# A graph attention layer on one core: the prologue as a written-out pipeline, the output in fifteen parts inside the batch loop, and the merge flags in PSUM

## The chip, the cores and the metric

One core of one Trainium2 chip runs the kernel; the other cores are idle. The metric is device time in microseconds (us) of one execution: the median of repeated runs without the profiler. One further execution was recorded by the hardware profiler, and every duration below that has a line beside it comes from that one.

The engines of the core have names used throughout: PE (matrix multiply, with its weight loads PEld), DVE (vector), ACT (scalar and activation), POOL (GpSimd) and SP (sync, here only a queue for DMA transfers). SBUF is the on-chip memory, PSUM the accumulator memory beside PE.

## The reference

A layer of graph attention with four heads of 32 columns over 12,500 nodes and 412,500 edges, sorted by their target `dst`:

```python
h = relu(layernorm(x))                          # 12500 x 128
hw = (h @ W_node.T).reshape(N, 4, 32)           # projected rows
e = (edge_attr_64 @ W_edge.T).reshape(E, 4, 32)
att = sum(concat([hw[src], hw[dst], e], -1) * a, -1)
att = where(att > 0, att, 0.2 * att)            # E x 4
m = maximum(segment_max(att, dst), 0)
ex = exp(att - m[dst])
denom = segment_sum(ex, dst) + (E - deg) * exp(-m)
out = x + segment_sum(ex / denom[dst] * hw[src], dst)
```

The term `(E - deg) * exp(-m)` counts every edge that does not end in the node as a zero.

## The kernel before

The kernel has three stages that follow each other.

**Prologue.** The 12,500 rows of `x` are handled as 98 blocks of 128 nodes (`NB`), seven blocks at a time (`GB`, lines L276 to L314): load, mean and variance (L289, L290), `rstd` and `shift` (L292 to L295), normalize with ReLU on ACT (L302), transpose on PE (L304) and copy to SBUF on DVE (L306), multiply by the weights on PE (L309), copy to `rows` on ACT (L310), write a constant one and keep the target's term `tn` on DVE (L312, L313), store 140 columns a node into the DRAM tensor `table` (L314). The same stage prepares tables on the edges. An edge chunk is 896 edges; there are 461 of them, padded to 464 (`NC2`). Its smallest target and whether it is sorted go through `ext` (L206 to L223), then some thirty DVE instructions on 464 columns make `floor`, `q0`, `new`, `lastm` and `nid` (L225 to L262), and POOL makes `key`, the place of each edge's target inside a window of 32 nodes, for all 3,248 columns at once (L265 to L274). A scheduler chooses the order on each engine here.

**Batches.** 58 batches (`NBT`) of eight chunks. In this stage the order is written by hand (`tc.manual_schedule()`), and each engine runs its own instructions strictly in that order. For batch b+1, POOL issues one indirect DMA for each tile of 128 edges (L364, `gather`), 3,223 in all, each fetching 128 rows of `table` into `hs`. They are issued in three groups a batch; a one-column POOL copy named `gate` (L360) makes each group wait until DVE and ACT have come to a certain point of batch b: the copy of chunk group 0 or 2 by ACT (L458), or the copy `r` (L473). For batch b, `weigh` (L402 to L426) makes the attention weights on DVE and ACT, `scatter` (L442 to L449) multiplies the gathered rows and sums them by target on PE; `begin` of batch b+1 (L377 to L396) compares targets (`mem`), multiplies the edge features (L382, L385) and builds the one-hot matrices `hot` from `key` (L393). After every second batch `merge` (L475 to L523) joins sixteen chunk results into the accumulator `acc` on DVE. SP loads each batch's edge features, targets and small tables.

**Rest.** `count_windows`, called in batch 3, counts the chunks that did not fit a window; a loop at the end (`window`, L794) redoes them, and runs no round on these inputs. Then `em` (L802 to L807) and, seven blocks at a time, `wgt`, PE, the sum with `x` and the store (L808 to L833) make the output.

Of the kernel before, what the change touches and what calls it, by code (L numbers as in the profile page):

```python
# [9 lines left out]
F32 = mybir.dt.float32  # L10
BF16 = mybir.dt.bfloat16
I32 = mybir.dt.int32
# [5 lines left out]
P = 128  # L18
# [23 lines left out]
GB = 7  # L42
FH = 2 * H
# [17 lines left out]
def filled(sc):  # L61

    return [T if c < NCH - 1 else LAST for c in (2 * sc, 2 * sc + 1) if c < NCH]

# [10 lines left out]
def kernel(  # L75
# [32 lines left out]
    key = const.tile([P, COLS], BF16, name="key")  # L108
    acc = const.tile([P, NQ, AW], F32, name="acc")
    nc.gpsimd.memset(acc, 0.0)  # L110
# [38 lines left out]
    def index(b):  # L149
        t = indices.tile([P, SB * CT], I32, name="src")  # L150
        nc.sync.dma_start(t, src[:, b * SB * CT:(b + 1) * SB * CT])
        return t

    early = [index(b) for b in range(2)]


    with (
        tc.tile_pool(name="prep1", bufs=1) as p1,
# [10 lines left out]
        dsts = p1.tile([P, COLS], I32, name="dsts")  # L169
        nc.scalar.dma_start(dsts, dst)  # L170
# [35 lines left out]
        for g in range(NG):  # L206
            n = min(P, NC2 - g * P)
            dch = p2.tile([P, CE], I32, name="dch")
            nc.sync.dma_start(dch[:n, :], dstc[g * P:g * P + n, :])
            nc.vector.tensor_reduce(ext[:n, g, 0:1], dch[:n, :], AX.X, OP.min)  # L210
            rise = p2.tile([P, CE - 1], I32, name="rise")
            nc.gpsimd.tensor_tensor(rise[:n, :], dch[:n, 1:], dch[:n, :CE - 1], op=OP.subtract)
            nc.vector.tensor_reduce(ext[:n, g, 1:2], rise[:n, :], AX.X, OP.min)
            pen = p2.tile([P, CE + 1], F32, name="pen")
            nc.gpsimd.memset(pen, -BIG)
            nc.vector.tensor_scalar(pen[:n, 1:CE], rise[:n, :], 0.0, -BIG, op0=OP.not_equal, op1=OP.mult)
            nc.sync.dma_start(pens[g * P:g * P + n, :], pen[:n, :])
        pb = [pps.tile([P, NC2], F32, name=f"pb{k}", bufs=1) for k in range(2)]
# [14 lines left out]

        floor = p1.tile([P, NC2], F32, name="floor")
# [24 lines left out]
        for a in range(4):  # L259
# [5 lines left out]
        dl = p1.tile([P, COLS], I32, name="dl")  # L265
        nc.vector.tensor_scalar(dl, dsts, W - 1, None, op0=OP.bitwise_and)
        rel = p1.tile([P, COLS], F32, name="rel")
        nc.gpsimd.tensor_copy(rel, dsts)
        nc.gpsimd.tensor_tensor(rel.rearrange("p (c t) -> p c t", t=T), rel.rearrange("p (c t) -> p c t", t=T),
                                floor[:, :, None].to_broadcast([P, NC2, T]), op=OP.subtract)  # L270
        nc.gpsimd.tensor_scalar(rel, rel, float(W), float(W), op0=OP.is_ge, op1=OP.mult)
        low_f = p1.tile([P, COLS], F32, name="dsts")
        nc.gpsimd.tensor_copy(low_f, dl)
        nc.gpsimd.tensor_tensor(key, rel, low_f, op=OP.add)  # L274

        for b0 in range(0, NB, GB):  # L276
            xg = p2.tile([P, GB, D], F32, name="xg")
            n = min(GB, -(-(N - b0 * P) // P))
            full = min(n, (N - b0 * P) // P)
            nc.sync.dma_start(xg[:, :full, :],  # L280
                              x[b0 * P:(b0 + full) * P, :].rearrange("(b p) d -> p b d", p=P))
            if full < n:
                nc.vector.memset(xg[:, full, :], 0.0)
                rest = N - (b0 + full) * P
                nc.sync.dma_start(xg[:rest, full, :], x[(b0 + full) * P:N, :])
            mv = p2.tile([P, GB, 2], F32, name="mv")
            for i in range(GB):
                stats = p2.tile([P, 6], F32, name="stats")
                nc.vector.bn_stats(stats, xg[:, i, :])  # L289
                nc.vector.bn_aggr(mv[:, i, :], stats)  # L290
            rstd = p2.tile([P, GB], F32, name="rstd")
            nc.scalar.activation(rstd, mv[:, :, 1], AF.Sqrt, bias=eps)  # L292
            nc.vector.reciprocal(rstd, rstd)
            shift = p2.tile([P, GB], F32, name="shift")
            nc.vector.scalar_tensor_tensor(shift, mv[:, :, 0], -1.0, rstd, op0=OP.mult, op1=OP.mult)  # L295
            rows = p2.tile([P, GB, ROW], F32, name="rows")
            for i0 in range(0, GB, 3):
                m = min(3, GB - i0)
                pt = pps.tile([P, 3, P], F32, name="pt")
                for i in range(i0, i0 + m):  # L300
                    hn = p2.tile([P, D], F32, name="hn", bufs=3)
                    nc.scalar.activation(hn, xg[:, i, :], AF.Relu, scale=rstd[:, i:i + 1],  # L302
                                         bias=shift[:, i:i + 1])
                    nc.tensor.transpose(pt[:, i - i0, :], hn, ident)  # L304
                hT = p2.tile([P, 3, P], F32, name="hT")
                nc.vector.tensor_copy(hT[:, :m, :], pt[:, :m, :])  # L306
                ph = pps.tile([P, 3, ROW], F32, name="ph")
                for i in range(m):
                    nc.tensor.matmul(ph[:, i, :], hT[:, i, :], wall, start=True, stop=True)  # L309
                nc.scalar.copy(rows[:, i0:i0 + m, :], ph[:, :m, :])  # L310
                ones = rows[:, i0:i0 + m, FH:].rearrange("p b (h k) -> p b h k", h=H)[:, :, :, HD]
                nc.vector.memset(ones, 1.0)  # L312
                nc.vector.tensor_copy(tn[:, b0 + i0:b0 + i0 + m, :], ph[:, :m, H:FH])  # L313
            nc.scalar.dma_start(table[b0 * P:(b0 + GB) * P, :].rearrange("(b p) c -> p b c", p=P), rows)  # L314


# [5 lines left out]
    bank = ps.tile([P, 2 * T * R + W], F32, name="exr")  # L322
    exr = [bank[:, k * T * R:(k + 1) * T * R].rearrange("p (t r) -> p t r", t=T) for k in range(2)]
    rows_ps = bank[:, 2 * T * R:]
# [48 lines left out]
    def begin(s):  # L373
# [9 lines left out]
        for part in (slice(0, HALF), slice(HALF, CE)):  # L383
            for k in range(2):
                nc.tensor.matmul(s.z[:, part], twb[:, s.b % 2, k, :], s.mem[:, k, part], start=False,  # L385
                                 stop=(k == 1))
        s.hot = []
        for j in range(SB):
            sc = s.b * SB + j
            if not tiles_of(sc):  # L390
# [3 lines left out]
                                    key[:, sc * CT:(sc + 1) * CT, None].to_broadcast([P, CT, W]),  # L394
# [80 lines left out]
    def merge(g, n):  # L475
# [34 lines left out]
        here = lastm[:, c0:c0 + n, :]  # L510
# [14 lines left out]
    def count_windows():  # L525
# [23 lines left out]
        nc.vector.tensor_copy(total, sum_f)  # L549
# [9 lines left out]

    with tc.manual_schedule():  # L560
        for b in range(-1, NBT):
            if b == -1:
                for k in range(2):
                    batch(k).src = early[k]
                load_pen(batch(0))
            elif b + 2 < NBT:
                batch(b + 2).src = index(b + 2)
# [8 lines left out]
            if b >= 0:  # L576
                s = batch(b)
                weigh(s)
                if b + 1 < NBT:
                    load_pen(batch(b + 1))  # L580
                s.pas = work.tile([P, BUF], F32, name="m")[:, :CB * H * AW].rearrange("p (c k) -> p c k", c=CB)
# [14 lines left out]
            if b == 3:  # L596
                count_windows()
    stack.close()
# [5 lines left out]
    neg_big = work.tile([P, 1], F32, name="neg_big")  # L604
    nc.vector.memset(neg_big, -BIG)
    ones = work.tile([1, P], F32, name="ones")
    nc.vector.memset(ones, 1.0)

    rsum = work.tile([P, P // W, W], F32, name="rsum")
    nc.vector.tensor_copy(rsum, rsame[:, None, :].to_broadcast([P, P // W, W]))  # L610

    tq = work.tile([P, NQ], F32, name="tq")
    for s in range(P // W):
        ptn = ps.tile([P, NB], F32, name="pz")
        for h in range(H):
            nc.tensor.matmul(ptn[h * W:(h + 1) * W, :], ident[s * W:(s + 1) * W, s * W:(s + 1) * W],
                             tn[s * W:(s + 1) * W, :, h], start=True, stop=True,
                             tile_position=(s * W, h * W))
        nc.vector.tensor_copy(tq.rearrange("p (b s) -> p b s", s=P // W)[:, :, s], ptn)

    def window():
# [9 lines left out]
        for i, row in enumerate([left_row] + rows):  # L631
# [6 lines left out]
                                       op0=OP.mult, op1=OP.add)  # L638
        vals = work.tile([1, 3], I32, name="vals")
        nc.vector.tensor_scalar(vals[:, 0:1], first, -1.0, float(NSC), op0=OP.mult, op1=OP.add)  # L640
# [151 lines left out]

    windows = nc.values_load(total[0:1, 0:1], min_val=0, max_val=NCH * NQ)
    with tc.For_i(0, windows, 1):  # L794
        window()


    stack.close()
    work = ctx.enter_context(tc.tile_pool(name="fin", bufs=2))
    ps = ctx.enter_context(tc.tile_pool(name="fin_ps", bufs=2, space=bass.MemoryType.PSUM))  # L800
    em = work.tile([P, NQ], F32, name="em", bufs=1)
    nc.scalar.activation(em, acc[:, :, AW - 1], AF.Exp, scale=-1.0)  # L802
    rest = work.tile([P, NQ], F32, name="rest", bufs=1)
# [65 lines left out]
```

## Time and profile before

| what | value |
|---|---|
| median of 3 runs | 5097.42 us (5096.45 to 5098.61) |
| profiled execution, own time | 4340.74 us |
| its span, first to last instruction | 4339.0 us |
| POOL busy | 3162.1 us (73%) |
| DVE busy | 1756.9 us (40%) |
| PE busy | 1260.8 us (29%) |
| ACT busy | 453.5 us (10%) |
| DMA moved | 434.48 MB |

The profiled execution is 756.68 us shorter than the median of the runs. Shares of busy time are averages over the three stages, which are limited by different things; the timeline is what separates them. DMA issue is not counted as busy, except that POOL's indirect DMAs are, since POOL works on each of them.

### The profile page before, as it was taken

The page shows a single profiled execution, that of the slowest core. Times are in us where ns is not written, and L with a number is a line of the kernel's source. Part 1 is how long each engine was busy: PE and PEld are TensorE (multiplying, and loading weights), DVE is VectorE, ACT ScalarE, POOL GpSimd, SP SyncE. Part 2 cuts the span into 40 slices and gives each one's busy share as a digit, 9 for nine tenths or more (in the row PEclk, how much of TensorE's full clock was granted, in tenths as well). Part 3 has the DMA queues.
Part 4 walks back from the last instruction along what each step waited for, and adds up shares of the span by engine and source line. Part 5 has one row for each costly group of instructions (what it writes and reads, how often), then busy time and mean ns, then how long its engine had stood idle before and what let it go on. Part 6 is the DMA issues. An engine that isn't in the chain of part 4 may idle for free. (4 is left out here: it accounts for less than half of the span.)

```text
span 4339.0 us, 30729 instructions
## 1 busy us (share of the span) xinstructions
PE 1260.8 (29%) x9107; PEld 535.4 (12%) x9107; DVE 1756.9 (40%) x3136; ACT 453.5 (10%) x1430; POOL 3162.1 (73%) x3422
## 2 busy tenths in 40 slices
PE   3613131313232222313131323232232313131324
PEld 2301010101011110101010101111010101010101
DVE  7325343444334342534343433434253434343346
ACT  2301010100101010101010000101010101010010
POOL 5277777777777777777777777777777777777771
PEclk8556565656555655556565656565655656565655
DMA  3433433333343334343343434343434333343434
GB/s 96 139 91 94 112 106 93 105 91 109 86 110 85 109 86 109 86 108 103 93 106 89 110 87 110 85 110 86 109 85 109 96 99 104 90 108 88 109 86 129
DMA packets 235471, 434.48 MB, mean 100 GB/s; under 512 B 85642, under 2 KB 135814, under 8 KB 235174
## 3 DMA queue, kind: packets, MB, share of 16 engines
q0 software_dynamic: 103136, 231.23, 23.5%
q1 hardware_dynamic: 118678, 192.44, 13.5%
q10 hardware_dynamic: 13488, 8.82, 0.6%
q8 instruction: 73, 1.20, 0.1%
q14 instruction: 96, 0.79, 0.1%
HBM read 417.15 MB, written 15.09 MB: 100 GB/s over the span
## 5 line engine op out<-in xcount | busy, mean ns | idle before, releaser
L364 POOL DMA_INDIRECT hs<-table,src x3223 | 3072.6, 953 | 1067.5 <-issue 1043.4
L449 PE MATMUL pa<-rhs,hot 128*32 128x140 f32 x6448 | 516.8, 430 | 2900.8 <-DVE rhs L444 2888.2
L402 DVE STREAM_TRANSPOSE zst<-hs 128x224 f32<-128x224 f32 x58 | 23.9, 412 | 1867.0 <-DMA hs<-table,src 1867.0
L449 PEld LDWEIGHTS pa<-rhs,hot 128*32 128x32 f32 x6448 | 271.4, 152 | 3148.3 <-issue 2740.1
L444 DVE TENSOR_TENSOR rhs<-hs,exr 128x924 f32<-128x924 f32 x461 | 515.0, 1117 | 151.2 <-ACT rhs L442 151.2
L382 PE MATMUL z<-eft,wa 128*32 128x384 f32 (+1 forms) x928 | 433.2, 627 | 16.2 <-DMA twb<-table 16.2
L411 ACT ACTIVATE a<-z 32x224 f32<-32x224 f32 x232 | 80.5, 347 | 2057.6 <-DVE z L410 2057.6
L385 PE MATMUL z<-mem,twb 128*32 128x512 f32 x464 | 186.7, 546 | 3.9 <-DMA twb<-table 3.9
L382 PEld LDWEIGHTS z<-eft,wa 128*32 128x32 f32 x928 | 119.1, 128 | 305.9 <-issue 300.1
L442 ACT COPY rhs<-exr 128x28 f32<-128x28 f32 x461 | 97.9, 212 | 332.3 <-DVE rhs L444 276.9
L420 ACT ACTIVATE both<-a 32x224 f32<-32x224 f32 x232 | 89.9, 388 | 376.3 <-DVE a L417 372.0
L393 DVE TENSOR_TENSOR hot<-exr,key 128x448 f32<-128x448 f32 x231 | 127.5, 611 | 0.0
L523 DVE TENSOR_TENSOR acc<-acc,a 128x70 f32 x461 | 109.7, 238 | 34.3 <-DVE acc L523 19.6
L458 ACT COPY m<-pa 128x280 f32<-128x280 f32 x231 | 90.5, 392 | 310.9 <-PE pa L449 310.9
L410 DVE TENSOR_TENSOR z<-z,zst 32x224 f32<-32x224 f32 x232 | 89.8, 387 | 77.9 <-ACT a L411 71.9
L416 DVE TENSOR_TENSOR_SCAN m<-pen,up 32x896 f32<-32x896 f32 x58 | 116.4, 2008 | 7.8 <-DVE up L414 0.5
L414 DVE TENSOR_TENSOR_SCAN up<-pen,z 32x896 f32<-32x896 f32 x58 | 117.0, 2017 | 2.0
L485 DVE TENSOR_SCALAR mc<-r 128x16 f32<-128x16 f32 (+1 forms) x29 | 5.6, 192 | 249.1 <-ACT r L473 249.1
L377 DVE TENSOR_SCALAR mem<-mem,nid 128x896 f32<-128x896 int32 x116 | 81.2, 740 | 26.3 <-DMA mem<-in_dstc 26.3
L422 DVE SCALAR_TENSOR_TENSOR both<-pen,m 32x224 f32<-32x224 f32 x232 | 88.7, 382 | 2.4
L473 ACT COPY r<-t 128x280 f32<-128x280 f32 (+1 forms) x58 | 23.7, 409 | 592.3 <-PE z L385 591.4
L467 PE MATMUL t<-m,rsame 128*32 128x280 f32 (+1 forms) x464 | 73.4, 415 | 0.4 <-ACT m L458 0.4
(142 smaller groups left out, 994.9 us busy)
## 6 DMA issues: line engine op xcount, KB each, us to landing
eft<-in_ef SPq DMA_DIRECT2D x58, 1792.0 KB
mem<-in_dstc SPq DMA_DIRECT2D x116, 448.0 KB
hs<-table,src POOLq DMA_INDIRECT x3223
xg<-in_x SPq DMA_DIRECT2D x26, 448.0 KB
twb<-table SPq DMA_DIRECT2D x464, 0.5 KB
table<-rows ACTq DMA_DIRECT2D x14, 490.0 KB
pen<-pens SPq DMA_DIRECT2D x58, 112.1 KB
out<-o SPq DMA_DIRECT2D x13, 448.0 KB
```

Source lines behind the costliest of these rows:

```text
L364: nc.gpsimd.indirect_dma_start(out=s.hs[:, i, :], out_offset=None, in_=table[:, :], in_offset=bass.IndirectOffsetOnAxis(ap=s.src[:, i:i + ...
L382: nc.tensor.matmul(s.z[:, part], wa3[:, j, :], s.eft[:, j, part], start=(j == 0), stop=False)
L385: nc.tensor.matmul(s.z[:, part], twb[:, s.b % 2, k, :], s.mem[:, k, part], start=False, stop=(k == 1))
L393: nc.vector.tensor_tensor(hot, rows_ps[:, None, :].to_broadcast([P, CT, W]), key[:, sc * CT:(sc + 1) * CT, None].to_broadcast([P, CT, W]), ...
L414: nc.vector.tensor_tensor_scan(up, s.pen[:, :CE], s.z, 0.0, op0=OP.add, op1=OP.max)
L416: nc.vector.tensor_tensor_scan(m[:, ::-1], s.pen[:, CE:0:-1], up[:, ::-1], 0.0, op0=OP.add, op1=OP.max)
L420: nc.scalar.activation(both[g * R:(g + 1) * R, 0, :, :], grouped(att, g), AF.Exp)
L442: nc.scalar.copy(rhs[:, :n, :, HD + 2], s.mx[:, :n, q * H:(q + 1) * H])
L444: nc.vector.tensor_tensor(rhs[:, :n, :, :HB], s.hs[:, i0:i0 + n, FH:].rearrange("p t (h d) -> p t h d", h=H), s.ex[:, :n, q * H:(q + 1) * ...
L449: nc.tensor.matmul(pa[g * W:(g + 1) * W, c, :], s.hot[j][:, c * T + i, :], rhs[:, i, :, :].rearrange("p h k -> p (h k)"), start=(i < 4), s ...
L458: nc.scalar.copy(s.pas[:, 2 * j:2 * j + n, :], pa[:, :n, :])
L523: nc.vector.tensor_tensor(cols, cols, put[:, i0 + i, :, :], op=OP.add)
```

## The change

*Prologue.* The block of L276 to L314 becomes a pipeline of 33 units of three blocks, in an order written out by hand. In step k of the loop DVE measures unit k+4, ACT and DVE make `rstd` and `shift` of unit k+3, ACT normalizes unit k+2, PE projects unit k and then transposes unit k+2, and ACT, DVE and a DMA keep unit k. `x` is loaded nine blocks at a time into four buffers, three loads ahead, by SP. The chunk tables (`extent`) are cut into pieces of one instruction and are put between the steps, one in every second step; the remaining pieces and the thirty instructions on 464 columns follow after the last step. The four loads of `dstc` move from SP's queue to ACT's. The clearing of `acc` on POOL moves behind POOL's first two pieces.

*Key.* The table `key` of all 3,248 columns and its POOL and DVE instructions go away, with their load; instead each batch loads its own 56 columns of `dst` (one more DMA on SP) and makes `key` in `begin` with four DVE instructions.

*Output.* `finish` makes the output of a part: thirteen parts of seven blocks, one of three and one of four. A part is issued after the `merge` of a batch given by `parts()`: batches 5, 9, 13, and so on to 53, then 55, and the last four blocks after batch 57. Its store is issued by SP in the next batch, after `load_pen`. The final loop of L808 is gone, and so are `em` and `rest` for all columns at once.

*One loop for what is left.* `count_windows` also checks that at each such batch the following chunk begins beyond the part (`need`); if one does not, or a chunk is left over, the loop at the end runs, and its last round makes all the output anew. `tq` and other constants of that loop move into its body.

*Merge flags.* `merge` copies its slice of `lastm` into a PSUM tile and uses that as an operand.

```diff
-        for b0 in range(0, NB, GB):
-            xg = p2.tile([P, GB, D], F32, name="xg")
...
+        while k < 0 or line:
+            u = next(units, None)
+            if u:
+                measure(u)
+            at = {j: v for j, v in line}
+            if k + 3 in at:
+                deviate(at[k + 3])
+            if k + 2 in at:
+                normalize(at[k + 2])
+            if k in at:
+                project(at[k])
+            if k + 2 in at:
+                turn(at[k + 2])
+            if k in at:
+                keep_rows(at[k])
+            line = [(j, v) for j, v in line if j > k]
+            if u:
+                line.append((k + 4, u))
+            if k == -2:
+                early = [index(b) for b in range(2)]
+            if k > 6 and k % 2:
+                next(extents, None)
+            k += 1
+        for _ in extents:
+            pass
...
-        rel = p1.tile([P, COLS], F32, name="rel")
-        nc.gpsimd.tensor_copy(rel, dsts)
...
-        nc.gpsimd.tensor_tensor(key, rel, low_f, op=OP.add)
...
+        dk = work.tile([P, SB * CT], I32, name="dk")
+        nc.vector.tensor_scalar(dk, s.dst, W - 1, None, op0=OP.bitwise_and)
+        key = work.tile([P, SB * CT], F32, name="key")
+        nc.vector.tensor_tensor(key.rearrange("p (c t) -> p c t", t=T), s.dst.rearrange("p (c t) -> p c t", t=T),
+                                floor[:, s.b * CB:(s.b + 1) * CB, None].to_broadcast([P, CB, T]), op=OP.subtract)
+        nc.vector.tensor_scalar(key, key, float(W), float(W), op0=OP.is_ge, op1=OP.mult)
+        nc.vector.tensor_tensor(key, key, dk, op=OP.add)
...
-        here = lastm[:, c0:c0 + n, :]
+        here = ps.tile([P, MC, 2], F32, name="t2")[:, :n, :]
+        nc.vector.tensor_copy(here, lastm[:, c0:c0 + n, :])
...
+    def finish(pool, psum, tag, bufs, em, b0, n):
+        q = slice(b0 * 4, (b0 + n) * 4)
...
+        nc.sync.dma_start(xg[:, :full, :], x[b0 * P:(b0 + full) * P, :].rearrange("(b p) d -> p b d", p=P))
...
+        nc.scalar.activation(em, acc[:, q, AW - 1], AF.Exp, scale=-1.0)
+        nc.vector.tensor_scalar(rest, acc[:, q, HD + 1], -1.0, float(E), op0=OP.mult, op1=OP.add)
+        nc.vector.tensor_tensor(em, em, rest, op=OP.mult)
+        nc.vector.tensor_tensor(em, em, acc[:, q, HD], op=OP.add)
+        nc.vector.reciprocal(em, em)
+        nc.vector.tensor_tensor(wgt[:, :n * 4, :], acc[:, q, :HD], em[:, :, None].to_broadcast([P, n * 4, HD]),
+                                op=OP.mult)
...
+            nc.vector.tensor_tensor(xg[:, :n, cols], po[:, :n, :], xg[:, :n, cols], op=OP.add)
...
+                for store in stores:
+                    store()
+                stores.clear()
...
+            for b0, n, last in parts():
+                if last == b:
+                    stores.append(finish(work, ps, "pa", 2, em_ps, b0, n))
```

## The prediction

> **What bounds the kernel now.** I read the busy slices first, then the costliest groups, the waits, and last the timeline at both ends of POOL's run. From the page's slices and groups:
>
> ```profile
> POOL 5277777777777777777777777777777777777771
> ...
> L364 POOL DMA_INDIRECT hs<-table,src x3223 | 3072.6, 953 | 1067.5 <-issue 1043.4
> ```
>
> Slices are 108.5 us. POOL is level in the batches and does little before 183 us and after 4248. A gather takes 0.95 us, and the timeline shows 0.30 between two, so one every 1.25. The longest waits answer whether anything else can hold the batches:
>
> ```profile
> DVE zst L402 <- DMA hs<-table,src: 1867.0, 58, 47.3
> ...
> POOL hs L364 <- issue: 1043.4, 3143, 110.4
> ...
> POOL gate L360 <- ACT rhs L442: 0.4, 1, 0.4
> ```
>
> DVE waits in each of the 58 batches for gathered rows; POOL practically never waits at its gate. Of POOL's 1043.4, 110.4 is one wait. The timeline (start, duration, engine, line) shows where:
>
> ```profile
> 53.99 11.51 POOL L271 TENSOR_SCALAR rel<-rel 128x3248 f32<-128x3248 f32 x1
> 54.39 11.18 DVE L261 TENSOR_SCALAR nid<-top,rcol 32x116 f32<-32x116 f32 x1
> ...
> 183.43 1.18 POOL L364 DMA_INDIRECT hs<-table,src  x1 [110.43 <-issue]
> ...
> 4247.09 0.95 POOL L364 DMA_INDIRECT hs<-table,src  x1 [0.30 <-issue]
> ...
> 4249.86 0.41 DVE L402 STREAM_TRANSPOSE zst<-hs 128x224 f32<-128x224 f32 x1 [11.71 <-DMA hs<-table,src]
> ...
> 4280.57 1.30 DVE L523 TENSOR_TENSOR acc<-acc,a 128x70 f32 x5 [0.61 <-DVE acc L523]
> ...
> 4286.56 0.92 ACT L802 ACTIVATE em<-acc 128x392 f32<-128x392 f32 x1 [13.12 <-DVEq L794]
> ...
> 4335.33 0.53 SPq L833 DMA_DIRECT2D out<-o  x1
> ```
>
> So 4339.0 = 183.4 (prologue, no gather) + 4064.6 (gathers) + 90.9 (last batch, then output). The last sum into `acc` ends at 4281.9; the output alone takes 57.1.
>
> **What the Trainium skill says.** "SBUF — State Buffer", SBUF: two separate sides: DVE in a two-port mode and GpSimd exclude each other for a whole instruction, and an indirect DMA from POOL starves while DVE holds the port, since POOL cannot write its descriptors. The trace agrees twice: `nid` on 32x116 takes 11.18 us beside L271 (its later fellow takes 0.31), and a gather beside L514 took 1.08 instead of 0.95. "VectorE: DVE Perf Modes", Why PSUM operands drop a tier: a PSUM operand keeps an instruction out of the two-port modes. No run shows that here yet. "DMA: Bandwidth & Descriptors", SWDGE vs HWDGE vs iDMA: transfers issued by SP and ACT are immune to that starvation; nothing before contradicts it.
>
> **The change part by part.** All against the profiled execution's own 4340.74; the median of the runs, 5097.42, is 756.68 higher, and no view says where that lies. I carry savings over at face value; stretched by 5097.42/4340.74 = 1.174 they would be a sixth larger.
>
> *1. Prologue, 183.4 before.* Groups of the first 184 us, for all 98 blocks: PE 54.4 (L309) + 36.3 (L304) = 90.7; DVE 23.7 + 15.1 (L289, L290) + 19.3 (L306) + 6.5 + 2.8 (L313, L312) + some 5 for `rstd` and `shift` = 72, and the extent pieces 4.2 + 4.3 + 2.5 = 11; ACT 41.9 (L302) + 17.4 (L310) + 33 x 0.30 = 69. PE is longest: 2.75 a unit, 91 in all. Each stage takes what was made a step or two earlier, so I let PE set the pace. First unit at 9, 7 to 13 (DVE's two dozen small instructions come ahead of it, and the first load must land: before, the first load was read at 12.65 behind some 2.5 MB of others, now it is SP's first), fill 5, PE 91, drain 2, and 3 where ACT's store issue waits for DVE's memset: 110. Then, uncovered, the last two extent pieces (1.1 + 0.6), the small matmuls (0.8) and the thirty instructions on 464 columns. Their rows, without the stretches beside POOL, sum to 12.9. That they count is a choice: `hs` lies where prologue tiles lay, and in the compiled program the first gather waits for the last `nid`. The last store of `table` lands beside them (before: issued at 178.0, gather at 183.4). First gather: 125. **-58**. Bounds: 115 if a faster PE clock leaves DVE's 83 as pace (9+5+83+2+15); 147 if a unit goes at the old pace, 7.7 for seven blocks, 3.3 for three (9+5+109+2+6 of extents+15). So -36 to -68.
> The key table's 31 us on POOL (11.5+7.4+6.2+2.9+2.9), largely in front of DVE's chain, goes with this; it is no second gain. Clearing `acc` (11.5) behind POOL's first pieces costs nothing: POOL waits for the table anyway. On SP, x loads now lead, and the early index loads follow the third; a store of `pens` that waits for DVE holds up the x load behind it, but x is three loads ahead, some 8 us each; ACT takes four `dstc` loads, 0.45 each to issue, while it waits for the first unit.
>
> *2. Key in each batch.* Four DVE instructions on 56 columns, nearest rows L490 and L511 at 0.17 to 0.21: 0.7 a batch in `begin`, 41 in all, inside DVE's idle (1867/58 = 32 a batch). `hot` is then 0.7 later, and `merge` behind it still waits 8 to 9 for ACT's `r`. To POOL they can cost at most their length, 41, if each shut it out wholly; L377 holds SBUF 1.3 a batch and lengthens gathers by some 0.3 where it strikes. I take +4, bounds 0 to +41. SP's extra DMA is 0.4 to issue; SP has idle time: it waits 1570 in all at L371 (`load_pen`).
>
> *3. Flags in PSUM.* One small copy (0.1) a merge; L514 keeps its 1.1 but, as the skill has it, lets go of the shared port. Gathers above their usual 0.947 sum to 24 over the run, some 10 of it beside L511 to L523: **-8**, bounds -10 to 0.
>
> *4. Output in the loop.* Parts 1 to 14: per part ACT 0.3, DVE about 0.8 for five small ones, 1.1 for `wgt` (L820), 4 x 0.32 (L830): 3.5, behind `merge`, in DVE's idle 19 to 23 us before the next `zst`; PE 1.9. Ahead of the gate nothing is added on DVE or ACT: after `zst` comes the same chain as before to the first L458, done 3.6 before the gate needs it (2109.03 and 2112.62 in batch 26). Stores stand on SP behind `load_pen`, when their sums are long done; SP then has some 40 us until the batch's small tables are needed. DMA, 38% busy in the batches, takes 13 MB more easily. So 0, bounds 0 to +15.
> Part 15 stays behind the last merge, on four blocks: ACT 0.3, small DVE 0.8, `wgt` 0.7, PE 0.5, sums 0.9, hand-overs 0.8: 4. Store: before, 4.1 from the last sum to the end; a second issue 0.5; the check of the loop and its barrier 2. So 10.5 stands for 57.1: **-46**, bounds -40 to -49. The `tq` copies (4281.9 to 4285.5) are within that.
>
> *5. The flag.* From the inputs, I computed q0 against need for the 14 parts with a following chunk: q0 leads by 2 to 12 columns of 32 nodes. The loop makes no round; the additions to `count_windows` are some 3 on an idle DVE.
>
> Sum: -58 + 4 - 8 - 46 = -108: 4233 in the profile, and 5097.4 - 108 = **4989**.
>
> **The rivals.**
> A. *The new DVE work starves POOL.* For it: [...]unprofiled gathers may be more exposed. Against: all such loss is 24 now. Key's whole 41, finish's 15, nothing from the flags: 5097 - 58 - 46 + 56 = 5049.
> B. *The pipeline keeps the old pace*, each step waiting for the slowest hand-over (DVE's in-order copy waits for PE, PE for ACT): first gather at 147; 5097 - 36 + 4 - 8 - 46 = 5011.
> C. *Slower: the late gate.* If `finish` or SP's longer queue put `weigh` back, POOL would stand at its gate in every batch. Price: the delay less 3.6, times 58. It eats the 108 from a delay of 3.6 + 1.9 = 5.5 a batch, and 7 gives 5097 - 108 + 197 = 5186. Against: the rows arrive last by 19 us or more.
> D. *It doesn't do what it says: the flag is set*, the loop makes a round, and all 14 pieces are made anew one after the other with one buffer: load 4.4, work 5, store 4.4 each, 14 x 14 = 193, and the round's own 40 (14 gathers 17.5, the rest a guess from one batch's chain): 5222. Against: the margins above.
>
> **How the numbers follow.** Main case 0.74, own range 4965 to 5015 (prologue bounds, stretch of a sixth); A 0.07; B 0.10; C 0.06; D 0.03. Range 4958 to 5050 holds main, B and A. A measurement can tell some 0.2%, 10 us: main, A and B are faster, 0.90; C with a delay just at its point gives 0.02 for no change; the rest, 0.08, slower.
>
> **What would show it.** Right: the first gather near 125, with DVE's `nid` just before it; PE with few gaps from 15 to 110; 3223 gathers at 1.26 or less from first to last; gathers beside the flags' products back at 0.95; the end some 12 after the last sum into `acc`. Wrong: a first gather after 150, gates that wait, gathers longer than 0.95 beside `key`, or a second output pass at the end.

## The result, and the profile after

The changed kernel takes 5246.35 us (median of 6 runs), the kernel before 5098.17 beside it: ratio 1.0291, 95% interval 1.0278 to 1.0304. It is slower by 148, where 108 less were forecast.

One thing must be known to read every number below. A sitting is a stretch in which a kernel and the kernel before are run in turn on one chip. The kernel before took 4322 to 4332 in some sittings and 5067 to 5101 in others, with nothing between. I call them **short** and **long** sittings. Its profile (4340.74) is 9 above the first kind and far from the second. The runs that the prediction was scaled to were long, the profile it was worked from was of the short kind. In a short sitting the change makes the kernel faster (e9: 4209.28 against 4328.83, 0.9723, interval 0.9707 to 0.9739), in a long one slower (above, and again in e4). All ratios here are within one sitting.

The profiled execution of the changed kernel (own time 5245.37, span 5243.6) is of the long sitting. Its page, busy slices and costliest groups:

```profile
POOL 2656556656656566566565665665656655656562
...
L446 POOL DMA_INDIRECT hs<-table,src x3223 | 3064.3, 951 | 1088.1 <-issue 1071.3
...
L442 POOL COPY gate<-m 128x1 f32<-128x1 f32 x114 | 21.7, 191 | 499.8 <-ACT rhs L532 487.3
...
L442 POOL COPY gate<-r 128x1 f32<-128x1 f32 x56 | 10.2, 183 | 476.0 <-DVE r L589 260.2
```

POOL stands at 5 to 6 tenths where it stood at 7. A gather is as long as before (951 ns); new is the idle time in front of `gate` (L442, before L360): 499.8 + 476.0. The waits (us in total, times, longest):

```profile
ACT m L548 <- remote: 2043.2, 117, 45.2
...
POOL hs L446 <- issue: 1071.3, 3194, 82.5
...
POOL gate L442 <- ACT rhs L532: 487.3, 56, 25.1
...
DVE zst L492 <- DMA hs<-table,src: 309.3, 15, 46.0
```

The two have changed places. DVE waited for gathered rows in all 58 batches (1867.0); now in 15 (309.3). POOL, which practically never waited at its gate, waits in every batch. ACT's copy `m` (L548), which opens a gate, waits 2043.2 for a release that the profile can't put to a recorded instruction ("remote"); what `m` reads comes from PE. The timeline at both ends:

```profile
110.25 1.29 DVE L394 TENSOR_SCALAR nid<-top,rcol 32x116 f32<-32x116 f32 x4
...
112.57 1.15 POOL L446 DMA_INDIRECT hs<-table,src  x1 [82.49 <-issue]
...
5189.09 0.95 POOL L446 DMA_INDIRECT hs<-table,src  x1 [0.30 <-issue]
...
5228.87 1.30 DVE L614 TENSOR_TENSOR acc<-acc,a 128x70 f32 x5 [0.61 <-DVE acc L614]
...
5234.84 0.42 SPq L687 DMA_DIRECT2D out<-xg  x1
```

So 5243.6 = 112.6 (prologue) + 5077.4 (gathers) + 53.6 (the rest). The prologue is 12 shorter than the forecast 125, the rest 9 longer than the forecast 45 (90.9 - 46); the gathers take 1013 more than the 4064.6 before. The stretch around a part of the output shows how (`xg` L682 are the sums of the part):

```profile
1066.89 0.18 POOL L442 COPY gate<-r 128x1 f32<-128x1 f32 x1 [9.18 <-DVE r L589]
...
1079.35 0.39 DVE L682 TENSOR_TENSOR xg<-pa,xg 128x224 f32<-128x224 f32 x1 [1.17 <-issue]
...
1079.79 0.97 PE L678 MATMUL pa<-a,ident 32*32 32x224 f32 x8 [0.47 <-DVE xg L682]
...
1088.20 0.39 DVE L682 TENSOR_TENSOR xg<-pa,xg 128x224 f32<-128x224 f32 x1 [8.46 <-remote]
...
1088.64 0.97 PE L678 MATMUL pa<-a,ident 32*32 32x224 f32 x8 [7.88 <-DVE xg L682]
1088.95 0.95 POOL L446 DMA_INDIRECT hs<-table,src  x1 [0.30 <-issue]
1093.19 0.69 DVE L682 TENSOR_TENSOR xg<-pa,xg 128x224 f32<-128x224 f32 x2 [4.60 <-remote]
1093.79 0.40 DVE L492 STREAM_TRANSPOSE zst<-hs 128x224 f32<-128x224 f32 x1
...
1111.12 0.18 POOL L442 COPY gate<-m 128x1 f32<-128x1 f32 x1 [21.23 <-ACT rhs L532]
...
1183.57 1.16 PE L539 MATMUL pa<-rhs,hot 128*32 128x140 f32 x14 [0.33 <-issue]
...
1194.12 0.39 ACT L548 COPY m<-pa 128x280 f32<-128x280 f32 x1 [11.84 <-remote]
...
1194.64 0.18 POOL L442 COPY gate<-m 128x1 f32<-128x1 f32 x1 [3.94 <-ACT rhs L532]
```

The r gate is the copy `gate` that reads `r`, an m gate one that reads `m`. Gathers flow from 1067, behind the r gate, to the one at 1088.95, the last before the m gate. PE's first products for the part are taken by DVE at once (1079.35), the next ones, done at 1080.8, only at 1088.20: the signal was 7.4 late. `zst`, the first work of DVE on gathered rows, stands behind these sums and goes at 1093.79, everything behind it moves, and the m gate opens 21.23 late. In the next batch, without a part, the same is seen at a smaller price: products of PE that ended by 1184.7 are seen by ACT at 1194.1, and the gate waits 3.94. In this execution signals of PE are prompt for some 12 us after the r gate, and then late, most of them until a few us after POOL has stopped. Behind the m gate, where POOL's pause is shorter, it comes sooner: products that PE ended at 1205.2, 10 us after gathers had begun again, are seen by ACT at 1226.4, while POOL is still at work. (The ends of PE's instructions are modelled. The starts on ACT and DVE are recorded, and in e9 below, read in the same way, no `m` starts more than 0.4 us after PE's products and ACT's own work before it are done.)

The changed kernel in a short sitting (e9), groups, waits and timeline:

```profile
POOL 2777777777777777777777777777777777777774
...
L446 POOL DMA_INDIRECT hs<-table,src x3223 | 3057.2, 949 | 1039.4 <-issue 1015.3
```

```profile
DVE zst L492 <- DMA hs<-table,src: 1746.3, 58, 47.1
```

```profile
113.00 1.15 POOL L446 DMA_INDIRECT hs<-table,src  x1 [82.69 <-issue]
...
4160.59 0.94 POOL L446 DMA_INDIRECT hs<-table,src  x1 [0.30 <-issue]
...
4194.27 1.30 DVE L614 TENSOR_TENSOR acc<-acc,a 128x70 f32 x5 [0.61 <-DVE acc L614]
...
4200.23 0.42 SPq L687 DMA_DIRECT2D out<-xg  x1
```

No wait at a gate, DVE waits for rows in all 58 batches, and the span of 4209.0 is 113.0 + 4048.5 + 47.5.

### The profile page after: what moved, and what is told of

Its sections match the earlier page's. It is cut to its first block, busy times and chain, and to the rows that moved or that the text cites. A ratio compares the mean times of both kernels' runs of the same rounds, so it can differ in the third digit from the quotient of the medians.

```text
span 5243.6 us, 31123 instructions
## 1 busy us (share of the span) xinstructions
PE 1427.6 (27%) x9107; PEld 523.6 (10%) x9107; DVE 1796.9 (34%) x3479; ACT 450.4 (9%) x1454; POOL 3119.1 (59%) x3417
## 4 chain that ended last, share of the span: by engine, by line
## 5 line engine op out<-in xcount | busy, mean ns | idle before, releaser
L539 PE MATMUL pa<-rhs,hot 128*32 128x140 f32 x6448 | 529.5, 438 | 2234.6 <-DVE rhs L534 1741.4
L464 PE MATMUL z<-eft,wa 128*32 128x384 f32 (+1 forms) x928 | 476.3, 662 | 92.8 <-issue 69.2
L442 POOL COPY gate<-m 128x1 f32<-128x1 f32 x114 | 21.7, 191 | 499.8 <-ACT rhs L532 487.3
L467 PE MATMUL z<-mem,twb 128*32 128x512 f32 x464 | 252.8, 641 | 216.9 <-issue 216.5
L442 POOL COPY gate<-r 128x1 f32<-128x1 f32 x56 | 10.2, 183 | 476.0 <-DVE r L589 260.2
L548 ACT COPY m<-pa 128x280 f32<-128x280 f32 x231 | 90.5, 392 | 2269.0 <-remote 2043.2
L678 PE MATMUL pa<-a,ident 32*32 32x224 f32 (+2 forms) x480 | 41.4, 550 | 620.2 <-issue 355.3
L492 DVE STREAM_TRANSPOSE zst<-hs 128x224 f32<-128x224 f32 x58 | 23.5, 406 | 311.5 <-DMA hs<-table,src 309.3
L614 DVE TENSOR_TENSOR acc<-acc,a 128x70 f32 x461 | 107.7, 234 | 34.2 <-issue 10.8
```

What stands on the lines that cost most here:

```text
L464: nc.tensor.matmul(s.z[:, part], wa3[:, j, :], s.eft[:, j, part], start=(j == 0), stop=False)
L539: nc.tensor.matmul(pa[g * W:(g + 1) * W, c, :], s.hot[j][:, c * T + i, :], rhs[:, i, :, :].rearrange("p h k -> p (h k)"), start=(i < 4), s ...
L548: nc.scalar.copy(s.pas[:, 2 * j:2 * j + n, :], pa[:, :n, :])
L614: nc.vector.tensor_tensor(cols, cols, put[:, i0 + i, :, :], op=OP.add)
```

## The experiments

Gate waits of a batch are read from the starts of its gathers: what lies between two beyond the usual 0.30.

**e0, the kernel before again.**

> The kernel before, unchanged, to see the profile of a run that takes 5097. Theory 1 (late gates): gathers still take 0.95 with 0.30 between two, first gather near 183, and the 757 us between 4340 and 5097 are POOL's waits at its gate copies (L360), some 13 a batch, because TensorE's signals reach ACT and DVE late while gathers flow. Theory 2 (slow gathers): the gate copies wait for nothing, and the gathers come every 1.50 us instead of 1.26.

4330.67: the sitting was short, no wait at the gates, gathers from 182.3 to 4237.9 and 91.0 after. It left open what the kernel before does in a long one; e11 answers that by subtraction only.

**e1 and e10, output behind the loop.** The edit, cut to its core:

```diff
-            for b0, n, last in parts():
-                if last == b:
-                    stores.append(finish(work, ps, "pa", 2, em_ps, b0, n))
...
+    em = work.tile([P, NQ], F32, name="em", bufs=1)
+    for b0 in range(0, NB, GB):
...
```

> The changed kernel with its output taken out of the loop again (the fifteen parts, their stores, the flag and the second pass go; the output of the kernel before follows the batches). Theory 1: each of 14 parts in the loop makes the next m gate wait 21.4 instead of 4.4, 17 x 14 = 238; the output behind the loop costs some 45 more than now. 5246 - 238 + 45 = 5053, 5030 to 5075. Theory 2 (the waits come from what every batch got: the key's four instructions, the second index load, the flags in PSUM): the parts cost nothing, 5246 + 45 = 5290.

> The changed kernel with its output behind the loop, run behind the changed kernel in the same sitting. Where the kernel before takes 4326: 4253. Where it takes 5098: theory 1a (each of fourteen parts costs 17 there) 5246 - 238 + 45 = 5053, 5030 to 5075; theory 1b (what every batch got) 5290. Theory 3: slow here, even if e8 was not.

Both sittings were short: 4253.15 (0.9832, 0.9815 to 0.9848) and 4254.04 (0.9825, 0.9809 to 0.9842). Prologue, key and flags together are worth some 73 to 75.

**e2, only the output in the loop**, all else as before.

> The kernel before with only the output in fifteen parts in the loop; prologue, key table and flags as before. Theory 1: 5097 + 238 - 37 = 5298, 5270 to 5320. Theory 2: 5097 - 37 = 5060.

4283.19 beside 4326.53 (0.9903, 0.9886 to 0.9919): 43 less. Neither theory's number, both of which were for a long sitting; the two halves sum to 116.

**e3, e7, e12, e14, each part one batch later.**

```diff
-                if last == b:
+                if min(last + 1, NBT - 1) == b:
```

> The changed kernel with each part made one batch later (parts 1 to 14; part 15 stays last), so behind a batch without a merge, shortly after the r gate has opened, not some 10 to 25 us after it. Theory 1a (TensorE's signals are prompt for the first 15 us or so after a gate and late after): a part's four hand-overs from TensorE to DVE are then mostly prompt, the extra wait falls from 17 to about 5: 5246 - 14 x 12 = 5078, 5050 to 5130. Theory 1b (a part costs what it takes on DVE, wherever it stands): 5246, within 20.

> The kernel with each part one batch later, once more, for a run where the kernel before takes 5098. Theory 1a: the four hand-overs of a part from TensorE to DVE then fall into the stretch after the r gate has opened, where signals are prompt: 5246 - 14 x 12 = 5078, 5050 to 5130. Theory 1b (a part costs its length wherever it stands): 5246. Where the kernel before takes 4326: 4214 again.

> The kernel with each part one batch later, for a sitting in which the kernel before takes 5070 to 5100. Theory 1a (TensorE's signals are on time for some 15 us after a gate has opened, late after that): a part's hand-overs then fall behind the r gate, where no merge stands ahead of them, and the extra wait of 17 at the next m gate falls to about 5: 5246 - 14 x 12 = 5078, 5050 to 5130. Theory 1b (a part costs the same wherever it stands): 5246, or 5217 beside 5070. Where the kernel before takes 4326: 4214 again.

> The kernel with each part one batch later, again for a sitting in which the kernel before takes 5070 to 5100. Theory 1a: 5246 - 14 x 12 = 5078 beside 5098, 5050 beside 5070, within 40. Theory 1b (a part costs the same wherever it stands): 5246 beside 5098, 5217 beside 5070. Where the kernel before takes 4326: 4212 again.

All four sittings were short: 4214.56, 4213.25, 4211.23 and 4213.39 beside 4324 to 4328. There the place makes little difference: in the one sitting that had both, the parts one batch later took 4214.93 (e8) and in place 4209.28 (e9). The question was settled by e16 and e17.

**e4, e8 and e9: does the changed kernel bring the late signals on?**

> The changed kernel, unchanged, beside new runs of the kernel before. In the first experiments the kernel before took 4326 with no wait at its gates, and its two halves of the change summed to 73 + 43 less. Theory 1 (the change itself is worth what the forecast's parts say, and loses only where TensorE's signals come late): where the kernel before takes 4326, the changed one takes 4326 - 73 - 43 = 4210, within 15, and its gates wait for nothing; where the kernel before takes 5097, 5246. Theory 2 (the changed kernel brings the late signals on by itself): about 5246 even beside 4326.

> The kernel with each part one batch later, run ahead of the changed kernel in the same sitting. So far the kernel before has taken 4326 wherever the changed kernel was not run beside it and 5098 wherever it was. Theory 1 (a sitting is slow or not, whatever runs in it): this one is as the rest of its sitting, 4214 beside 4326 or about 5078 (5050 to 5130) beside 5098. Theory 3 (the changed kernel leaves something behind that slows what runs after it): 4214 here, ahead of it.

> The changed kernel, unchanged, between two others. Theory 1: 4210, within 15, where the kernel before takes 4326, and 5246 where it takes 5098. Theory 2 (the changed kernel brings the late signals on by itself): 5246 whatever the others take.

e4 met a long sitting: 5247.84 against 5098.51 (1.0295, 1.0277 to 1.0312). e8, e9 and e10 shared a short one: 4214.93, 4209.28, 4254.04 beside 4328.83. The same changed kernel has no late signals there, and nothing slows behind it. So theories 2 and 3 fall; in every sitting here all kernels were of one kind, short or long.

**e5 and e13, slower gathers.** POOL gets two copies of one column behind every gather.

```diff
+            for _ in range(2):
+                nc.gpsimd.tensor_copy(pace, eps)
```

> The changed kernel with two small copies of a constant on POOL behind every gather, so that gathers come every 1.50 us or so instead of 1.25. In the trace of the changed kernel at 5246, TensorE's signals come on time for some 15 us after a gate opens and then late until a few us after POOL stands still[...]. Theory 1a (the lateness comes of the pace of the gathers): at 1.50 the signals are on time and the gates wait for almost nothing: 112.6 + 3223 x 1.51 + 54 = 5033, faster than 5246 although POOL has more to do. Theory 1b (TensorE is late by itself, whatever POOL does): the gates wait less by what POOL loses, 5246 or more. Where the kernel before takes 4326, both say 5033.

> The changed kernel with two small copies of a constant on POOL behind every gather, for a sitting in which the kernel before takes 5070 to 5100; in a sitting at 4326 it took 5324, with 1.60 from gather to gather and no wait at the gates. Theory 1a (the lateness of TensorE's signals comes of the pace of the gathers): at 1.60 the signals are on time, and it takes 5324 again, within 20. Theory 1b (TensorE is late by itself, whatever POOL does): POOL's added 0.34 x 3223 = 1100 eat up the 1040 of gate waits only where they stand in the same stretch; the hand-overs stay late and waits at the gates stay, 5450 or more.

Short sittings: 5323.86 and 5325.56. My 5033 was wrong by the size of the copies: e13's groups are

```profile
L447 POOL DMA_INDIRECT hs<-table,src x3223 | 3166.1, 982 | 603.2 <-issue 153.8
L451 POOL COPY pace<-eps 128x1 f32<-128x1 f32 x6446 | 1245.7, 193 | 211.4
```

The gap between two gathers grew from 0.30 to 0.59, a gather from 0.95 to 0.98, and with a few longer gaps one comes every 1.60. On what makes signals late they say nothing; e16 does.

**e6, output behind the loop and flags from SBUF.**

```diff
-        here = ps.tile([P, MC, 2], F32, name="t2")[:, :n, :]
-        nc.vector.tensor_copy(here, lastm[:, c0:c0 + n, :])
+        here = lastm[:, c0:c0 + n, :]
```

> The changed kernel with the output behind the loop, as in the kernel before, and the merge's products reading the flags from SBUF again: the new prologue and the key in the batches are left. Where the kernel before takes 4326: 4253 + 8 by the forecast's price of the flags, 4251 to 4263. Where it takes 5098: theory 1 (the fourteen parts cost 17 each there) gives 5246 - 238 + 45 = 5053, 5030 to 5075; theory 2 (what every batch got) 5290.

4252.59 beside 4326.04, 0.9833 (0.9817 to 0.9850), where e1 and e10 with the flags in PSUM had 0.9832 and 0.9825. The flags are worth nothing that can be measured in a short sitting, the only kind that e6 met.

**e11, output behind the loop in a long sitting.**

> The changed kernel with its output behind the loop, for a sitting in which the kernel before takes 5098. Theory 1a (there each of fourteen parts makes the next m gate wait 17 longer): 5246 - 238 + 45 = 5053, 5030 to 5075, faster than before. Theory 1b (what every batch got makes the gates late): 5246 + 45 = 5290. Where the kernel before takes 4326: 4253 again.

4994.24 beside 5069.52: 0.985 (0.9833 to 0.9866), faster than before by 75, as much as in the short sittings. Theory 1b falls. 5053 was for a sitting at 5098; e11 is 30 lower than 5053 less the 29 between the sittings. Its waits show the loop without the parts:

```profile
POOL gate L442 <- DVE r L589: 257.1, 28, 9.3
POOL gate L442 <- ACT rhs L532: 234.0, 56, 23.3
POOL gate L442 <- ACT r L563: 188.1, 28, 8.2
```

The m gates (ACT `rhs`) waited 487.3 with the parts and wait 234.0 without: 253 for fourteen parts, 18 each. The r gates wait 445 instead of 476, so a part costs at most 20 in all. The two traces are from sittings 29 apart, and part of these 284 can be that. Beside its own kernel before, the changed kernel is 148 slower, e11 is 75 faster although its end is 37 longer, so the fourteen parts cost 148 + 75 + 37 = 260, 19 each. The gate waits that are left, 743 by the gaps between the gathers, are what the kernel before must have too: 5069.5 - 1.7 - 182.3 - 4055.5 - 91.0, with e0's stretches, leaves 739. That is by subtraction; its own profile in a long sitting was not caught.

**e15 and e16, four stretches in one kernel.** Batches 0 to 13 unchanged, 14 to 27 with the parts one batch later, 28 to 41 with slower gathers, 42 to 57 without the m gates.

```diff
+            for _ in range(2 if 28 < s.b <= 42 else 0):
+                nc.gpsimd.tensor_copy(pace, eps)
...
-                        gather(batch(b + 1), 1 + j // 2, s.pas[:, 2 * j, 0:1])
+                        gather(batch(b + 1), 1 + j // 2, s.pas[:, 2 * j, 0:1] if b < 42 else None)
...
-                if last == b:
+                if last + (14 <= last < 28) == b:
```

> The changed kernel with four stretches of batches in one run: 0 to 13 unchanged; 14 to 27 with their three parts one batch later; 28 to 41 with two small copies on POOL behind every gather (1.60 from gather to gather); 42 to 57 without the m gates. Where the kernel before takes 4326: no waits in the first three, 4209 + 780 x 0.34 = 4475, within 30. Where it takes 5070 to 5100, by stretch. Theory 1a (TensorE's signals come late when gathers have flowed for some 15 us at 1.25): some 13.5 of gate waits a batch and 17 more a part in the first; about 5 a part instead of 17 in the second; no gate waits in the third; about 28 a batch at the r gate in the fourth, since POOL then gives TensorE no pause between 0 and 69 us. Theory 1b (TensorE is late by itself, whatever POOL does): 17 a part in the second as in the first; late signals still in the third; in the fourth the waits of a batch sum to 13.5 as before, at one gate instead of two.

> The four stretches again, for a sitting in which the kernel before takes 5070 to 5100: unchanged, parts one batch later, slower gathers, no m gates. Theory 1a: 13.5 a batch and 17 more a part; about 5 a part; no gate waits; about 28 a batch at the r gate. Theory 1b: 17 a part in the second stretch too; late signals still in the third; in the fourth the waits of a batch sum to 13.5. Where the kernel before takes 4326: 4479 again.

e15 met a short sitting: 4479.23, no waits at the gates where they stand. e16 met a long one: 5351.81 beside 5069.01 (1.0558, 1.0528 to 1.0589). POOL's waits in it, in the windows 700 to 1326, 1509 to 2505, 2859 to 3847 and 3943 to 5121, which lie in the four stretches in this order:

```profile
POOL gate L443 <- ACT rhs L535: 60.0, 7, 21.0
POOL gate L443 <- DVE r L592: 37.0, 4, 9.3
...
POOL gate L443 <- DVE r L592: 57.6, 6, 11.0
POOL gate L443 <- ACT rhs L535: 46.0, 12, 4.1
...
POOL hs L447 <- issue: 14.1, 17, 1.5
...
POOL gate L443 <- ACT r L566: 163.1, 6, 28.9
POOL gate L443 <- DVE r L592: 111.9, 4, 28.1
```

First stretch, by batch and without the first six (the sixth, behind `count_windows`, has 35.9): 11 to 14 of gate waits, and 31 in each of the three behind a part. Second: 11 to 14, once 15.8; the batches behind its three parts have 11.6 to 11.9, so a part that cost some 17 costs nothing there (I had said 5). Third: no gate waits. Fourth: 25.8 to 29.9 at the r gate alone, as forecast from a POOL that gives PE no pause for 69 us. Theory 1b fails in the second and the fourth. In the third, missing gate waits alone would not refute it: a batch takes 89 to 91 us there instead of some 82 to 84, and that could hide signals that are late all the same. What ACT's `m` waits for decides it, in the first window and in the third:

```profile
ACT m L551 <- remote: 208.7, 12, 43.7
...
ACT m L551 <- PE pa L542: 31.5, 29, 2.4
```

In the third no wait of `m` is put down to "remote", none is longer than 2.4, and 2.4 is also its longest wait for PE in e9. So the signals themselves are on time there, and 1b fails in all three. The granted clock is no rival: it is 0.55 in the first window and 0.57 in each of the others, late or not. In a long sitting PE's signals are late when gathers flow at one per 1.25 us; at 1.60, with two small copies between them, they are on time. This rests on one profiled execution in a long sitting, with some fourteen batches to a stretch.

**e17, parts one batch later, a whole run in a long sitting.**

> The kernel with each part one batch later, for a whole run in a sitting in which the kernel before takes 5070 to 5100. In the four stretches, beside 5069, three parts made a batch later added nothing to the gate waits of their batches, where three in place had added 17 to 22 each. Theory 1a: as with the output behind the loop (4994 beside 5069), less what the output at the end takes more (some 37): 4957 beside 5069 or 4986 beside 5098, within 20. Theory 1b (what the stretch showed does not carry to all fourteen): above 5050. Where the kernel before takes 4326: 4212 again.

4981.23 beside 5069.87: 0.9824 (0.9808 to 0.9841), 24 above the forecast of 4957 and 4 outside its margin. Its waits at the m gates:

```profile
POOL gate L442 <- ACT rhs L532: 252.1, 56, 26.0
```

They are back from 487.3 to near e11's 234.0. The sums `xg` of the parts waited 173.6 us for "remote" in the changed kernel, 9.6 at the longest, and wait 52.9 here, 5.9 at the longest. A part now also has no `merge` ahead of it on DVE; how much of the gain is that, and how much the prompter signals, was not separated. Against e11 the gate waits are 26 more in all, 6 of it in batch 44 and the rest spread, and the end is 35 shorter. So this version beats the kernel before in both kinds of sitting (0.974 and 0.982), which the changed kernel does in one.

## Why the prediction was wrong

**The failed step is the carrying over.** The prediction worked everything against an execution of 4340.74, saw that the runs lie 756.68 higher "and no view says where that lies", and still took the covers of that execution for those of the runs. By the subtraction under e11 the 757 is gate waits: in the runs that it was scaled to, POOL stands at its gates some 13 us in each batch, and the slack of 3.6 before the gate does not exist. The honest answer to an unexplained 757 would have been a range with that case in it.

**Step 4, the parts inside the loop: forecast 0 (0 to +15), measured about +260 in a long sitting, no gate wait in a short one.** "In DVE's idle 19 to 23 us before the next `zst`" was the cover; in a long sitting most of that idle time is gone (`zst` waits 714.3 in e11, without the parts, and 309.3 with them, instead of 1867.0), the sums `xg` wait for PE, and `zst` stands behind them. The end of the kernel: forecast -46, measured 91.0 to 47.5, so -43.5 (e9 against e0), and e2 as a whole -43.

**Rival C had the mechanism and too small a chance (0.06).** It said that `finish` could put `weigh` back and make POOL stand at its gate; its evidence against, rows that arrive last by 19 us, was true of the profile only. Its price, the same delay in all 58 batches, was not what came: some 19 in each of 14.

**Step 1, the prologue: forecast -58, measured 182.3 to 113.0, -69.** The step let PE set the pace. In 10 to 97 us of e9 DVE is the busiest, 73 of 87 us, and PE only 63, at a granted clock of 0.82 to 0.97; before, it was 0.57 over most of that work (107.7 to 178.5 us). That DVE sets the pace is read from this and was not tested. It is the bound that the step named for a faster clock, taken as the end of the range and not as its middle (its terms add up to 114, given as 115, and those of the other bound to 146, given as 147). `nid` is the last thing ahead of the first gather, as said.

**Step 2, the key: +4 forecast.** In e6, with the key in the batches and the flags in SBUF, the gathers take 4048.1 from first to last, 4055.5 in e0. No loss; e1 with 4059.4 shows how far single profiles scatter.

**Step 3, the flags: -8 forecast, nothing measured** (e6 against e1 and e10). It rested on the Trainium skill, "VectorE: DVE Perf Modes", Why PSUM operands drop a tier, which says that a PSUM operand keeps an instruction out of the modes that take both SBUF ports; if that holds for these products, what it frees is below what these runs can tell.

**Step 5, the loop for what is left:** no second output pass appears in the timeline; in e9 the end is 13.4 behind the last sum into `acc` (4209.0 - 4195.6), forecast at some 12.

In a short sitting the sum of -108 meets a measured -120: -69 + -7 in the gathers + -44 at the end. It is nearer than its terms: the prologue gave 11 more than forecast, the flags none of their 8, and the -7 lies within the scatter of the profiles. In a long one -70 - 37 at the ends stand against 1030 of gate waits instead of some 768: +155 before the 7 of the gathers, and 148 measured. The 768 comes from subtraction, so that this adds up is no check of it.

## What to carry over

When a profile and the runs differ by more than their scatter, find where the difference lies before using any cover from the profile, or treat the covers as unknown. A chain that hands work from PE to DVE in the middle of a continuous stream of gathers is the part to distrust: place it right behind a point where the stream has paused, or outside the loop. Here the same fourteen parts cost some 260 behind the merge and some 26 one batch later, in long sittings.

## What the runs showed of the hardware

Two kinds of sitting differ by 17 to 18% for the kernel before (5069 and 5098 against 4326) and by 25% for the changed one (5246 against 4209), at the same length of a gather (0.95 in the changed kernel in both) and similar granted clocks (the kernel before: 0.591 to 0.599 beside e15, 0.568 to 0.572 beside e17). The chip alone doesn't decide: two of the chips, 10 and 15, met sittings of both kinds. The long sittings lie at two levels, 5098 (the result and e4) and 5069 (e11, e16, e17). In the long ones what comes from PE is held up once gathers have flowed for a while, and SP with it: of SP's 443 recorded waits in the changed kernel, 103 took over 0.3 us, 68 of them about 0.70, against 8 of 443 in e9, none of them about 0.70. In the same traces most records of landed DMAs are missing: 12,919 in the changed kernel's profile, 63,433 in e9's. In e16, 2.6 a us are there in the first stretch and 10.4 in the third, where gathers are slower and signals on time (e15: 15.5 and 12.2). So the lateness and the missing records go together. Whether one queue holds both up, whether the recording itself plays a part, and what makes a sitting long, is open: no run here tells it. On the recording in particular: every run of the record has a span and a granted clock of its own, and the profiled execution counts among them, so none of these runs is known to be free of recording, although they are called runs without the profiler above.
